# A graph network's layer-norm statistics merged, one copy moved from ScalarE to VectorE, and the instructions of all engines in a new order

## The chip, the cores and the metric

The kernel runs on one core of a Trainium2 chip. The metric is the device time of one execution in microseconds (us); several executions give a median. A separate, profiled execution left the trace that the views below read.

TensorE (PE) multiplies matrices, VectorE (DVE) and ScalarE (ACT) work element by element, GpSimd (POOL) does the powers of the layer norms, and SyncE (SP) starts most of the DMAs.

## The reference

64 graphs of 256 nodes with 256 features go through four layers. Every layer begins with a layer norm and a relu, and adds its result to its input. Layers 0 to 2 are graph attention (four heads, four heads with bias, relu and a norm of each head, and one head), layer 3 is a GRU of three steps over the neighbours' messages.

```python
h = jnp.maximum(_layernorm(x, axis=-1), 0.0)
x = x + _L0_gnn_ref(h, adj, ...)      # attention, 4 heads of 64, elu
h = jnp.maximum(_layernorm(x, axis=-1), 0.0)
x = x + _L1_gnn_ref(h, adj, ...)      # attention, 4 heads of 64, bias, relu, norm per head
h = jnp.maximum(_layernorm(x, axis=-1), 0.0)
x = x + _L2_gnn_ref(h, adj, ...)      # attention, 1 head of 256
h = jnp.maximum(_layernorm(x, axis=-1), 0.0)
x = x + _L3_gnn_ref(h, adj, ...)      # 3 GRU steps:
# m = h @ weight[i]; aggr = A^T @ m; r, z = sigmoid(..); n = tanh(i_n + r * h_n)
# h = (1 - z) * n + z * h
def _layernorm(x, axis=-1, eps=1e-5):
    m = jnp.mean(x, axis=axis, keepdims=True)
    v = jnp.var(x, axis=axis, keepdims=True)
    return (x - m) / jnp.sqrt(v + eps)
```

## The kernel before, in words

**Units.** The work comes in 33 units: the first and the last hold one graph, the 31 between hold two. A unit's rows are cut into chunks of 128 nodes (four for two graphs), and `graphs` (L1027) describes a unit's layers one after the other. `vec` (L879) wraps most VectorE operations and some of ScalarE's, so these all stand on L880 in the profile (L906 in the changed kernel) and are told apart by their tiles.

**Norm (L1041).** For each chunk VectorE takes `bn_stats` (L1048, six numbers per row: count, mean and spread of the even and of the odd elements) and `bn_aggr` (L1049, mean and variance). In layers 0 to 2 a small VectorE operation makes the row of negative means, ScalarE subtracts the mean and takes the relu (`xn`, L1063), another small one adds eps, and GpSimd's power makes the reciprocal root, which is applied later to the projected rows. Ahead of the GRU (`whole`) ScalarE's relu has the reciprocal root as its scale (L1069).

**Attention.** `xn` is transposed, by TensorE (L1104, units 0 to 2 and 32) or by DMA: ScalarE splits it into two planes of 16 bits (L1119), a transposing DMA turns the planes, and ScalarE joins them (L1125). TensorE projects (L1143). For each head `weights` (L1234) makes the attention's weights `pt`: in the plain form VectorE does four passes (L1240) and one minimum with the mask `cap`, over 128x1024; a head named in `LIFTED` has four ScalarE passes (L1249) and four shorter VectorE passes instead, but only in units of two graphs. TensorE then attends, two heads of 64 on half arrays (L1275, 128x64) or one head of 256 on the whole array.

**GRU (L1448).** TensorE's gates (L1492) multiply the state `ht` by `whh`, and the aggregated state `ag` by `wc`; ScalarE and VectorE make the gates from the banks. `split` (L1454) cuts a tile into a high and a low part, `hl`, and `aggregate` (L1464) multiplies both by the adjacency (L1471). Between two GRU steps the state is turned to rows, by TensorE (L1529) or, in units 1 to 31 for the first of the two 128-column halves and for both after the last step, in `rows_turned` (L1499): ScalarE splits planes (L1508), a DMA transposes them to `tp`, ScalarE joins them to `y` (L1513). `y` goes into `split` between steps, or is added to `xt` after the last.

**The order.** Every operation is first recorded with an engine, a cost in ns, and what it reads and writes. `_Schedule` (L555) then plays the engines through at build time. Due times are counted back from `sched.end` of a unit (L1603, a graph is given `PACE`/2), each engine takes the earliest due operation that is ready and has room in its pools, and `HOP` is the margin after an engine's operation before others may use its result. What it decides is the fixed order of the instructions on each engine and of the pools' slots; on the chip the instructions of an engine run in that order, and wait on semaphores.

Of the kernel before, what the change touches and what calls it, by code (L numbers as in the profile page):

```python
# [14 lines left out]
OP = mybir.AluOpType  # L15
# [509 lines left out]
BACK = range(1, 32)  # L525
EARLY = (0,)
LIFTED = (0,2)
LEAVE = 0
PACE = 98000.0

# [17 lines left out]
class _Op:  # L548
    __slots__ = (
        "engine", "cost", "port", "emit", "group", "bufs", "takes", "nbytes", "succs", "waits", "due", "ready",  # L550
        "index", "yields", "base", "grabs", "leave",
    )


class _Schedule:  # L555
# [11 lines left out]
    OVERLAP = {"pe": 0, "act": 97, "dve": 81, "pool": 0, "sp": 0}  # L567
    HOP = {"pe": 300, "act": 100, "dve": 200, "pool": 100, "sp": 0}
    DMA_LATENCY = 3500
# [5 lines left out]
    YIELD = 5000.0  # L575
    GUARDED = ()
    STRICT = ("hl",)

    def __init__(self, tc, pools):
# [11 lines left out]
    def op(self, engine, cost, emit, reads=(), writes=(), takes=(), nbytes=0, port=False, yields=False,  # L591
           grabs=False, leave=0):
        o = _Op()
        o.leave = leave
        o.port, o.yields, o.grabs = port or grabs, yields, grabs
        o.engine, o.base, o.emit, o.group, o.nbytes = engine, cost, emit, self.group, nbytes
        o.cost = cost * self.RESERVE.get(engine, 1.0)
        o.succs, o.index, o.ready = [], len(self.ops), 0.0
        deps, o.bufs, o.takes = set(), [], []
        for written, items in ((False, reads), (True, writes)):  # L600
            for item in items:
                b, part = item if isinstance(item, tuple) else (item, None)
                if b not in o.bufs:
                    o.bufs.append(b)
                    b.left += 1
                if written and b.tile is None and b not in o.takes:
                    o.takes.append(b)
                keys = list(b.parts) if part is None else [k for k in (part, None) if k in b.parts]
                for k in keys:
                    writer, readers = b.parts[k]  # L610
                    if writer is not None:
                        deps.add(writer)
                    if written:
                        deps.update(readers)
                writer, readers = b.parts.get(part, (None, []))
                if written:
                    if part is None:
                        b.parts.clear()
                    b.parts[part] = (o.index, [])
                else:  # L620
                    b.parts[part] = (writer, readers + [o.index])
        for b in takes:
            if b.tile is None and b not in o.takes:
                o.takes.append(b)
        deps.discard(o.index)
        o.waits = len(deps)
        for d in deps:
            self.ops[d].succs.append(o)
        self.ops.append(o)
        return o  # L630
# [55 lines left out]

    def run(self):
        ops = self.ops
        for o in reversed(ops):
            late = self.end[o.group]  # L690
            for s in o.succs:
                if s.group == o.group or o.group not in self.end or o.group < 0:
                    late = min(late, s.due - self.STRETCH * s.cost - self.MARGIN)
            if o.nbytes:
                late -= self.DMA_LATENCY + o.nbytes / self.DMA_RATE
            o.due = late
        self.started = set()
        self.takers = {c: [] for c in self.pools}
# [7 lines left out]
        clock = self.dma_free = self.port_free = 0.0  # L706
        kept, holder = False, None
        count = 0
# [14 lines left out]
        while True:  # L723
            for e in engines:
# [5 lines left out]
                if e == "pool":  # L730
                    kept = False
                while able[e]:
                    item = heapq.heappop(able[e])
                    o = ops[item[1]]
                    free = not o.port or self.port_free <= clock and not (o.yields and kept)
                    if e == "dve" and o.port and kept and spare(o.due + self.YIELD):
                        free = False
                    if o.yields and holder == "pool" and clock < self.port_free <= clock + 200:
                        free = True
                    if e == "pool" and not free and self.roomy(o):  # L740
                        kept = True
                    if free and self.roomy(o):
                        self.start(o, clock)
                        idle[e] = False
                        free = clock + o.cost - self.OVERLAP[e]
                        post(free, "free", o)
                        if o.grabs:
                            self.port_free, holder = clock + 100, e
                            post(clock + 100, "tick", o)
                        elif o.port and not (o.yields and self.port_free > clock):  # L750
                            self.port_free, holder = free, e
                            post(free - 200, "tick", o)
                        break
                    held.append(item)
                for item in held:
                    heapq.heappush(able[e], item)
# [27 lines left out]
def _fast_path(  # L784
# [242 lines left out]
    def graphs(u, first, nb):  # L1027
# [13 lines left out]
        def norm(xt, cls, whole):  # L1041
# [4 lines left out]
            def stats(c):  # L1046
# [3 lines left out]

                op("dve", 615, emit, [(xt, c)], [(st, c), (mv, c)])

# [3 lines left out]
            def centred(c):  # L1056
                to, view = part(c)
                if c in CENTRED:
                    vec(nc.vector.tensor_scalar, 410, view, lambda: xt.tile[:, c, :],
# [3 lines left out]
                op("act", 505, lambda: nc.scalar.activation(  # L1063
                    view(), xt.tile[:, c, :], AF.Relu, bias=mv.tile[:, 3, c : c + 1],
                ), [(xt, c), (mv, "b")], [to])

# [7 lines left out]
            for c in range(C):  # L1074
                stats(c)
            if not whole and not all(c in CENTRED for c in range(C)):
                vec(nc.vector.tensor_scalar, 150, lambda: mv.tile[:, 3, :], lambda: mv.tile[:, 0, :], -1.0, None,
                    op0=OP.mult, reads=parts(mv, range(C)), writes=[(mv, "b")])
            if not whole:
                for c in range(C):  # L1080
                    centred(c)
            vec(nc.vector.tensor_scalar, 150, lambda: mv.tile[:, 2, :], lambda: mv.tile[:, 1, :], 1e-5, None,
                op0=OP.add, reads=parts(mv, range(C)), writes=[(mv, "r")])
            vec(nc.gpsimd.tensor_tensor, 220 + 195 * C, lambda: mv.tile[:, 2, :], lambda: mv.tile[:, 2, :],
                nhalf[:, :C], op=OP.pow, writes=[(mv, "r")], engine="pool", grabs=True)
            if whole:
                vec(nc.vector.scalar_tensor_tensor, 160, lambda: mv.tile[:, 3, :], lambda: mv.tile[:, 0, :], -1.0,
                    lambda: mv.tile[:, 2, :], op0=OP.mult, op1=OP.mult,
                    reads=parts(mv, range(C)) + [(mv, "r")], writes=[(mv, "b")])
                for c in range(C):  # L1090
                    scaled(c)
            return xns, mv

        def transposed(xns, cls):
# [18 lines left out]
            def turned(b):  # L1113
                pl, tp = buf("pl", [P, 2, 2 * D], U16), buf("tp", [P, 2, 2 * D], U16)

                def planes(flat):
                    return flat.bitcast(U16).rearrange("p (n k) -> p k n", k=2)

                op("act", 1040, lambda: nc.scalar.copy(  # L1119
                    pl.tile, planes(xns[b].tile.rearrange("p c d -> p (c d)"))), [xns[b]], [pl])  # L1120
                dma("sp", 1 << 18, lambda: nc.sync.dma_start(
                    tp.tile.rearrange("p k (m n) -> p (k m) n", n=P), pl.tile.rearrange("p k n -> p (k n)"),
                    transpose=True,
                ), [pl], [tp], cost=1250)
                op("act", 1330, lambda: nc.scalar.copy(  # L1125
                    planes(ht.tile[:, 2 * b : 2 * b + 2].rearrange("p c d n -> p (c d n)")), tp.tile,
                ), [tp], [(ht, b)])

# [105 lines left out]
        def weights(cap, f, cbs, h):  # L1234
# [21 lines left out]

            if h in LIFTED and nb == 2:
                for b in range(nb):
# [21 lines left out]
        def attend_heads(o, o_view, pts, wh, hs):  # L1280
# [8 lines left out]

            op("pe", pe(958) * len(hs), emit, [*pts, wh], banks_, takes=[o])  # L1290

# [156 lines left out]
        def gru(pair):  # L1448
# [5 lines left out]
            def split(src, turned, reads, port=False):  # L1454

                hl = buf("hl", [P, 2, C, P] if turned else [P, 2, 2, D], F32R)
                op("act", act(590) if turned else 590,
                   lambda: nc.scalar.copy(hl.tile[:, 0], src()), reads, [(hl, 0)])  # L1458
                vec(nc.vector.tensor_tensor, dve(683) if turned else 683, lambda: hl.tile[:, 1], src,
# [39 lines left out]
            def rows_turned(ht, j, last):  # L1499
# [5 lines left out]
                def planes(flat):  # L1505
                    return flat.bitcast(U16).rearrange("p (n k) -> p k n", k=2)

                op("act", 1040, lambda: nc.scalar.copy(pl.tile, planes(ht.tile[:, j, :])), [(ht, j)], [pl])  # L1508
                dma("sp", 1 << 18, lambda: nc.sync.dma_start(
                    tp.tile.rearrange("p k (m n) -> p (k m) n", n=P), pl.tile.rearrange("p k n -> p (k n)"),  # L1510
                    transpose=True,
                ), [pl], [tp], cost=1250)
                op("act", 1330, lambda: nc.scalar.copy(  # L1513
                    planes(y.tile.rearrange("p c d -> p (c d)")), tp.tile), [tp], [y])
                if not last:
# [161 lines left out]
```

## Time and profile before

| | us |
|---|---|
| median of 3 runs | 3011.49 (3011.26 to 3012.68) |
| profiled execution: its own time | 3010.84 |
| its span | 3009.0 |
| TensorE (PE) busy | 2972.5 |
| ScalarE (ACT) busy | 2435.3 |
| VectorE (DVE) busy | 2286.4 |
| GpSimd (POOL) busy | 295.5 |

The largest groups of instructions say what each engine's time consists of. A line of this view names the code's line, the engine, the operation, the tile written and the tiles read, the shapes and the count; then the busy time in all, the mean of one in ns, and the idle time before.

```profile
L1492 PE MATMUL bank<-ag,wc 128*128 128x512 f32 (+1 forms) x2376 | 1061.6, 581 | 0.0
L1492 PE MATMUL bank<-ht,whh 128*128 128x512 f32 (+1 forms) x2376 | 1059.7, 580 | 0.8 <-ACT ht L880 0.8
L1275 PE MATMUL bank<-wh,pt 128*64 128x65 f32 (+1 forms) x8704 | 375.7, 232 | 1.7 <-ACT f L1229 1.2
L1048 DVE BATCH_NORM_STATS2 st<-xt 128x6 f32<-128x256 f32 x512 | 207.5, 405 | 5.9 <-DMA xt<-in_x_dram 5.9
L1049 DVE BATCH_NORM_AGGREGATE mv<-st 128x2 f32<-128x6 f32 x512 | 94.0, 184 | 19.9
L1513 ACT COPY y<-tp 128x1024 uint16<-128x1024 uint16 x124 | 163.9, 1334 | 0.0
```

Two thirds of TensorE's time are the GRU's gates. A group's busy time can be below count times mean, since instructions overlap a little. The chain of work that ended last is followed back from the last instruction; the windows give every engine's busy time in a stretch, and the clock granted to TensorE; the waits name what TensorE stood idle for; the timeline shows single instructions, or runs of them, with start and duration.

### The profile page before, as it was taken

To read this page: it belongs to the slowest core of one execution; us is meant where nothing else is said; L and a number is where in the kernel's file an instruction comes from. 1 tells how busy PE (TensorE), PEld (TensorE's weight loads), DVE (VectorE), ACT (ScalarE), POOL (GpSimd) and SP (SyncE) were. 2 spreads that over 40 slices of the span, in tenths; PEclk is the share of its full clock that TensorE was granted. 3 is DMA by queue.
4 is the path that set the end of the run, shared out by engine and by line. 5 is a ranking of instruction groups with operands and counts; after the bars stand their busy time and mean duration, and the time that the engine had idled before them with its cause. 6 is when DMAs were issued, how large, how long until landed. Compare 5 with 4: busy or idle time off the path is not lost.

```text
span 3009.0 us, 47645 instructions
## 1 busy us (share of the span) xinstructions
PE 2972.5 (99%) x17175; PEld 1780.5 (59%) x17175; DVE 2286.4 (76%) x5510; ACT 2435.3 (81%) x4445; POOL 295.5 (10%) x317
## 2 busy tenths in 40 slices
PE   8899999999999999999999999999999999999998
PEld 6765656556556555565556565555565555555556
DVE  7878877778877778777788777788777788777754
ACT  7877888878789797888878888787897978877654
POOL 2101000111100101010010100111001010100000
PEclk9999999999999999999999999999999999999999
DMA  4222333333333333333333234233333333322210
GB/s 137 67 67 58 88 74 85 92 65 92 73 86 94 78 78 75 91 79 81 84 71 96 67 85 101 59 92 78 88 85 81 78 74 86 69 60 67 46 37 19
DMA packets 494793, 232.12 MB, mean 77 GB/s; under 512 B 421642, under 2 KB 474452, under 8 KB 494548
## 3 DMA queue, kind: packets, MB, share of 16 engines
q1 hardware_dynamic: 490576, 227.62, 32.9%
q8 instruction: 138, 2.26, 0.3%
q10 hardware_dynamic: 3972, 1.36, 0.2%
q14 instruction: 107, 0.88, 0.1%
HBM read 109.84 MB, written 17.34 MB: 42 GB/s over the span
## 4 chain that ended last, share of the span: by engine, by line
PE 97%; DVE 2%; ACT 1%; DMA 0%; issue 0%; SPq 0%; ACTq 0%; DVEq 0%
PE bank L1492 66%; PE bank L1275 12%; PE bank L1143 11%; PE bank L1471 6%; PE bank L1529 1%; PE bank L1000 0%; PE bank L1198 0%; DVE o L880 0%; PE bank L1104 0%; DVE g L880 0%; DVE pt L880 0%; PE bank L1178 0%; DMA w0e<-in_L_gnn_W_dram 0%; DVE pt L1240 0%; ACT pt L1249 0%; DVE ht L880 0%
## 5 line engine op out<-in xcount | busy, mean ns | idle before, releaser
L1492 PE MATMUL bank<-ag,wc 128*128 128x512 f32 (+1 forms) x2376 | 1061.6, 581 | 0.0
L1492 PE MATMUL bank<-ht,whh 128*128 128x512 f32 (+1 forms) x2376 | 1059.7, 580 | 0.8 <-ACT ht L880 0.8
L1492 PEld LDWEIGHTS bank<-ag,wc 128*128 128x128 f32 x2376 | 444.6, 190 | 476.1 <-issue 451.3
L1492 PEld LDWEIGHTS bank<-ht,whh 128*128 128x128 f32 x2376 | 440.1, 191 | 470.8 <-issue 444.3
L880 ACT ACTIVATE g<-bank,bg 128x512 f32<-128x512 f32 (+1 forms) x594 | 393.1, 670 | 188.9 <-PE bank L1492 185.3
L880 DVE SCALAR_TENSOR_TENSOR g<-g,g 128x512 f32<-128x512 f32 (+1 forms) x396 | 266.3, 673 | 323.9 <-ACT g L880 322.2
L1275 PEld LDWEIGHTS bank<-wh,pt 128*64 128x64 f32 (+1 forms) x8704 | 343.5, 141 | 80.5 <-issue 58.3
L1275 PE MATMUL bank<-wh,pt 128*64 128x65 f32 (+1 forms) x8704 | 375.7, 232 | 1.7 <-ACT f L1229 1.2
L1249 ACT ACTIVATE pt<-cb,f 128x256 f32<-128x256 f32 x620 | 325.9, 591 | 0.4 <-PE bank L1275 0.4
L1125 ACT COPY ht<-tp 128x1024 uint16<-128x1024 uint16 x232 | 303.4, 1340 | 0.1
L880 DVE SCALAR_TENSOR_TENSOR pt<-pt,f,cap 128x256 f32<-128x256 f32 x620 | 275.0, 485 | 35.2 <-ACT pt L1249 34.5
L880 POOL TENSOR_TENSOR mv<-mv,nhalf 128x4 f32<-128x4 f32 (+1 forms) x132 | 142.0, 1076 | 1189.7 <-DVE mv L880 1178.6
L1471 PE MATMUL bank<-am_r,hl 128*128 128x256 f32 x1536 | 241.6, 307 | 0.7 <-ACT hl L1458 0.5
L1119 ACT COPY pl<-xn 128x1024 uint16<-128x1024 uint16 x232 | 233.9, 1040 | 0.0
L1471 PEld LDWEIGHTS bank<-am_r,hl 128*128 128x128 f32 x1536 | 198.8, 190 | 47.4 <-issue 37.3
L880 ACT ACTIVATE g<-g,bg 128x512 f32<-128x512 f32 (+1 forms) x198 | 139.3, 705 | 106.1 <-DVE g L880 105.8
L880 POOL TENSOR_TENSOR mean<-mean,nhalf 128x8 f32<-128x8 f32 (+1 forms) x66 | 134.9, 2063 | 788.2 <-DVE mean L880 755.5
L1048 DVE BATCH_NORM_STATS2 st<-xt 128x6 f32<-128x256 f32 x512 | 207.5, 405 | 5.9 <-DMA xt<-in_x_dram 5.9
L1153 ACT ACTIVATE wh<-bank,mv 128x264 f32<-128x264 f32 (+1 forms) x384 | 172.0, 479 | 43.1 <-PE bank L1143 41.6
L880 DVE SCALAR_TENSOR_TENSOR g<-ht,g 128x512 f32<-128x512 f32 (+1 forms) x198 | 132.4, 670 | 85.3 <-ACT g L880 85.1
L1240 DVE TENSOR_SCALAR pt<-cb,f 128x256 f32<-128x256 f32 x532 | 188.2, 410 | 6.5 <-ACT cb L1186 3.2
L880 DVE SCALAR_TENSOR_TENSOR g<-bank,g 128x512 f32<-128x512 f32 (+1 forms) x198 | 133.2, 673 | 72.5 <-PE bank L1492 67.0
(97 smaller groups left out, 3333.7 us busy)
## 6 DMA issues: line engine op xcount, KB each, us to landing
cb<-rd SPq DMA_DIRECT2D x120, 512.0 KB, 4.9
xt<-in_x_dram SPq DMA_DIRECT2D x31, 512.0 KB, 4.1
at<-in_adj_dram SPq DMA_DIRECT2D x31, 512.0 KB, 3.8
out_dram<-xt SPq DMA_DIRECT2D x31, 512.0 KB, 3.0
cb<-rd SPq DMA_DIRECT2D x34, 256.0 KB, 3.3
tp<-pl SPq DMA_TRANSPOSE x356, 3.1
cap<-cap_n SPq DMA_TRANSPOSE x128, 2.4
rd<-row ACTq DMA_DIRECT2D x60, 8.0 KB, 1.3
```

The lines of the kernel that those rows point to most:

```text
L880: emit = lambda: fn(*[a() if callable(a) else a for a in args], **kw)
L1048: nc.vector.bn_stats(st.tile[:, c, :], xt.tile[:, c, :])
L1119: op("act", 1040, lambda: nc.scalar.copy(pl.tile, planes(xns[b].tile.rearrange("p c d -> p (c d)"))), [xns[b]], [pl])
L1125: op("act", 1330, lambda: nc.scalar.copy(planes(ht.tile[:, 2 * b : 2 * b + 2].rearrange("p c d n -> p (c d n)")), tp.tile,), [tp], [(ht, b)])
L1143: nc.tensor.matmul(ps.tile[:, : heads * W], lhsT=ht.tile[:, c, dc, :], rhs=we[:, dc].rearrange("p h w -> p (h w)"), start=(dc == 0), stop= ...
L1153: op("act", 470, lambda: nc.scalar.activation(wh.tile[:, :, c, :], ps.tile[:, : heads * W].rearrange("p (h w) -> p h w", h=heads), AF.Iden ...
L1240: nc.vector.tensor_scalar(pt.tile[:, b, jc, :].rearrange("p (i n) -> p i n", n=P), cb.tile[:, k, 2 * b : 2 * b + 2, :], f.tile[:, 1, h, c ...
L1249: op("act", 590, lambda: nc.scalar.activation(view().rearrange("p (i n) -> p i n", n=P), cb.tile[:, k, 2 * b : 2 * b + 2, :], AF.Relu, sca ...
L1275: nc.tensor.matmul(ps[q * Q : (q + 1) * Q], lhsT=pt.tile[:, b, jc, i0 : i0 + Q], rhs=wh.tile[:, h, 2 * b + jc, :w], start=(jc == 0), stop= ...
L1471: nc.tensor.matmul(ps.tile[:, b * N : (b + 1) * N], lhsT=rows(k, b, sc), rhs=am.tile[:, 2 * b + sc, :], start=(k == 0 and sc == 0), stop=( ...
L1492: nc.tensor.matmul(by_chunk(ps.tile[:, :S]), lhsT=w[:, dc, g * P : (g + 1) * P], rhs=block(v, dc), start=(first and dc == 0), stop=(last a ...
L1529: nc.tensor.transpose(ps.tile[:, c * P : (c + 1) * P], ht.tile[:, j, c * P : (c + 1) * P], ident)
```

## The change

Four things are done.

1. `MERGED`: no `bn_aggr`. The spread and the means of the halves are merged for all chunks at once, by five small VectorE operations: the bias row (minus the sum of the two means, so that the relu takes twice `xt`), and four that give the variance with eps.
2. `JOIN_DVE = ("y",)`: the 124 joins of `y` are VectorE copies. The splits into planes, and the joins of `ht`, stay on ScalarE.
3. `LIFTED0 = (0,)` with `HEADS = 3`: units 0 to 2 lift head 0 alone, and units of one graph lift as well.
4. The planner: `HOP` of VectorE 60 ns for 200, `PACE` 97000 for 98000, pools `wh` and `cb2_` guarded, and the attends marked as `halves`, so that among TensorE operations of equal due time one of the same kind as the last is preferred (`STICK` and `SWITCH` are zero). The order of the instructions changes on every engine.

```diff
+HEADS = 3
+LIFTED0 = (0,)
+JOIN_DVE = ("y",)
+MERGED = True
 LIFTED = (0,2)
 LEAVE = 0
-PACE = 98000.0
+PACE = 97000.0
...
-    HOP = {"pe": 300, "act": 100, "dve": 200, "pool": 100, "sp": 0}
+    HOP = {"pe": 300, "act": 100, "dve": 60, "pool": 100, "sp": 0}
...
-    GUARDED = ()
+    GUARDED = ("wh","cb2_")
     STRICT = ("hl",)
+    STICK = 0.0
+    SWITCH = {True: 0.0, False: 0.0}
...
+                if MERGED:
+                    vec(nc.vector.bn_stats, 405, lambda: st.tile[:, c, :], lambda: xt.tile[:, c, :],
+                        reads=[(xt, c)], writes=[(st, c)])
+                else:
+                    op("dve", 615, emit, [(xt, c)], [(st, c), (mv, c)])
+
+            def merged():
+                m0, q0, m1, q1 = (st.tile[:, :, k] for k in (1, 2, 4, 5))
+                d, s, v = (mv.tile[:, k, :] for k in range(3))
+                share = 1.0 / D if whole else 4.0 / D
+                stt = nc.vector.scalar_tensor_tensor
+                nc.vector.tensor_tensor(d, m0, m1, op=OP.subtract)
+                stt(s, q0, 1e-5 * D, q1, op0=OP.add, op1=OP.add)
+                stt(d, d, 0.25 if whole else 1.0, d, op0=OP.mult, op1=OP.mult)
+                stt(v, s, share, d, op0=OP.mult, op1=OP.add)
...
                 op("act", 505, lambda: nc.scalar.activation(
                     view(), xt.tile[:, c, :], AF.Relu, bias=mv.tile[:, 3, c : c + 1],
+                    scale=2.0 if MERGED else 1.0,
                 ), [(xt, c), (mv, "b")], [to])
...
+            if MERGED:
+                vec(nc.vector.scalar_tensor_tensor, 165, lambda: mv.tile[:, 3, :], lambda: st.tile[:, :, 1], -1.0,
+                    lambda: st.tile[:, :, 4], op0=OP.mult, op1=OP.subtract,
+                    reads=parts(st, range(C)), writes=[(mv, "b")])
...
+            if MERGED:
+                op("dve", 560, merged, parts(st, range(C)), [(mv, "r")])
...
+        def planes_op(by_dve, cost, to, of, reads, writes):
+            if by_dve:
+                vec(nc.vector.tensor_copy, 690, to, of, reads=reads, writes=writes, port=True)
+            else:
+                op("act", cost, lambda: nc.scalar.copy(to(), of()), reads, writes)
...
-            if h in LIFTED and nb == 2:
+            if h in (LIFTED if u >= HEADS else LIFTED0):
...
-            op("pe", pe(958) * len(hs), emit, [*pts, wh], banks_, takes=[o])
+            op("pe", pe(958) * len(hs), emit, [*pts, wh], banks_, takes=[o], halves=True)
...
-                op("act", 1330, lambda: nc.scalar.copy(
-                    planes(y.tile.rearrange("p c d -> p (c d)")), tp.tile), [tp], [y])
+                planes_op("y" in JOIN_DVE, 1330, lambda: planes(y.tile.rearrange("p c d -> p (c d)")),
+                    lambda: tp.tile, [tp], [y])
```

## The prediction

> **What bounds the kernel now.** I read the page's busy shares and its chain first, then the table of windows, TensorE's waits, and its timeline where it idles.
>
> ```profile
> PE 2972.5 (99%) x17175; PEld 1780.5 (59%) x17175; DVE 2286.4 (76%) x5510; ACT 2435.3 (81%) x4445; POOL 295.5 (10%) x317
> PE 97%; DVE 2%; ACT 1%; DMA 0%; issue 0%; SPq 0%; ACTq 0%; DVEq 0%
> ```
>
> TensorE is busy for 2972.5 of 3009.0 us and is 97% of the chain. The windows show where the other 36.5 us lie:
>
> ```profile
> 25.00:50.00 25.00, 24.44 (x287) 20.75 (x288) 21.24 (x73) 24.18 (x72) 3.31 (x5) 1.00 0.38 110
> 75.00:100.00 25.00, 15.78 (x305) 14.09 (x304) 23.64 (x65) 21.14 (x60) 2.28 (x4) 0.94 0.38 96
> 100.00:125.00 25.00, 24.21 (x120) 21.07 (x120) 23.06 (x63) 18.71 (x48) 4.60 (x5) 0.85 0.07 22
> ...
> 1410.00:1504.00 94.00, 94.00 (x533) 55.22 (x533) 71.18 (x173) 83.26 (x159) 8.02 (x10) 1.00 0.40 92
> 2820.00:2914.00 94.00, 91.94 (x403) 49.66 (x403) 58.76 (x143) 56.79 (x90) 5.34 (x7) 1.00 0.21 49
> 2914.00:3008.00 94.00, 84.80 (x329) 55.84 (x327) 35.16 (x75) 39.87 (x72) 0.80 (x2) 0.99 0.08 20
> ```
>
> Columns: length, busy time of TensorE, its loads, VectorE, ScalarE, GpSimd; then the clock. From 282 to 2820 us TensorE never idles. Of the start's 24.2 us idle (first 300 us), 9.2 fall between 75 and 100 us, where VectorE is busy 23.64 of 25, and the clock stands at 0.94 and 0.85. The end has 11. The waits and the timeline name the causes:
>
> ```profile
> PE bank L1104 <- ACT xn L1063: 9.4, 1, 9.4
> PE bank L1104 <- ACT xn L1069: 7.5, 1, 7.5
> ...
> 99.79 1.18 PE L1104 MATMUL bank<-ident,xn 128*128 128x128 f32 x4 [7.47 <-ACT xn L1069]
> 101.77 3.78 PE L1492 MATMUL bank<-ht,whh 128*128 128x256 f32 x8 [0.79 <-ACT ht L880]
> ```
>
> The first GRU gate, 8 matmuls of 256 columns, starts at 101.77 and takes 3.78 us; the same form takes 1.89 later: half clock, recorded from 97.1 to 107.3 us. So VectorE and ScalarE bound about 100 us, TensorE's work bounds 2700, latency the last 100. A mean load of 76% and 81% says little; only what shortens the start, the end or TensorE's own work moves the time.
>
> **Part by part.** *Statistics.* 512 aggregates (184 ns) and 231 TENSOR_SCALAR (164 ns) go: 94.2+37.9 = 132.1 us. Five small passes for each of 132 norms come: 660 at the 165 ns of the same small rows = 108.9. By durations VectorE saves 23 us. Here a rule speaks against the change: the Trainium skill ("VectorE: DVE Perf Modes", "Rules for kernel authors") counts operations, since each empties the pipe. For four chunks that is 10 before and 9 after (10 and 10 in the norm ahead of the GRU): almost nothing. The trace shows more than a count:
>
> ```profile
> 15.13 0.41 DVE L1048 BATCH_NORM_STATS2 st<-xt 128x6 f32<-128x256 f32 x1
> 15.58 0.18 DVE L1049 BATCH_NORM_AGGREGATE mv<-st 128x2 f32<-128x6 f32 x1
> 15.68 0.39 DVE L1048 BATCH_NORM_STATS2 st<-xt 128x6 f32<-128x256 f32 x1
> 16.11 0.18 DVE L1049 BATCH_NORM_AGGREGATE mv<-st 128x2 f32<-128x6 f32 x1
> ```
>
> A pair repeats every 0.55 us, because the aggregate starts only when its statistics have ended; operations that don't feed each other follow at their duration less 0.08, here 0.32. So before: 4×0.55+2×0.08 = 2.36; after: 3×0.32+0.46 (a dependent start) + about 0.6 for five = 2.0. I take 0.35 us of queue per norm, 46 in all; by the rule it is 10 or less. Neither shows in the middle, where VectorE is loaded to 75%.
>
> *Joins.* 124 copies `y<-tp` leave ScalarE (1.334 us, 165.4 in all). VectorE has no row for them. Nearest below: the one-source cast `am_r<-am`, 128x1024, 0.695; nearest above: the two-source `pt<-pt,cap`, 128x1024, 1.226. The skill's same page ("What auto-detection actually checks") gives double rate to one source between two SBUF tiles with even outer dimensions, as here; but ScalarE needs 1.340 to write 2-byte values apart against 1.040 to read them so, and VectorE might pay too. I take 0.69, nearest in kind: +86 us; by the upper row +152. Behind the wait for the transposed planes stand the GRU's VectorE passes, and behind those TensorE's banks; a transpose lands 3.1 us after issue, and the order allows for 4.7. Cover: between the end of `hl<-y,hl` and its aggregate I find 0.73, 0.98, 1.64 and 2.01 us, so even 1.226 (0.54 over the plan) stays covered.
>
> *Heads.* Units 1 and 2 drop head 2's ScalarE lift in two layers: 4×(4×0.410+1.226−4×0.485) = +3.7 us VectorE, −9.4 ScalarE. Eight one-graph heads gain it: −4.3, +9.5. Sums: VectorE 2286−23+86−1 = 2348 (78%; at most 2414, 80%), ScalarE 2435−165 = 2270 (75%). In the middle both stay under TensorE.
>
> *New order, middle.* TensorE's instructions are as many and of the same forms. Runs between the half-array attends (128*64) and the rest fall from 181 to 155. The timeline prices one:
>
> ```profile
> 1423.37 1.88 PE L1492 MATMUL bank<-ht,whh 128*128 128x512 f32 x4
> 1425.18 3.95 PE L1275 MATMUL bank<-wh,pt 128*64 128x65 f32 x128
> 1429.07 1.98 PE L1492 MATMUL bank<-ag,wc 128*128 128x512 f32 x4
> 1430.89 1.45 PE L1492 MATMUL bank<-ht,whh 128*128 128x512 f32 x3
> ```
>
> From start to start the gate before the attends takes 1.81 us and the one after 1.82, against 1.716 between gates elsewhere: 0.1 a switch, 26×0.1 = −2.6. The planner's VectorE margin falls from 200 to 60 ns, so products come sooner after what they wait for: TensorE's work between a unit's `ag` and its product is at least 1.71 us (1.73 before), for `hl` 2.66 (2.58), for the transposes of `ht` 3.45 (3.93); those of `wh` mostly 1.71 instead of 3.43, a distance at which before has no idle. I take +1 for stalls, bounds 0 and +10.
>
> *Start.* TensorE's first matmul waits on ScalarE's first relu (table load); unchanged. Ahead of the split for the first aggregate (real start 102.70) VectorE's queue holds 84.8 us of work in before, 78.1 in after (every instruction ahead in the order, by its form's time from start to start), and 18.4 of idle. If that idle stays, the split comes at 96.5 and the first gate near 97; if DMA or ScalarE set it, at 101; if all queues shorten alike (ScalarE's is 81.4, then 72.3), at 94. Counted in the same way TensorE has 63.55 us of work before that gate, in after 61.6 (four projections of unit 3, 3.56 us, now stand inside the gap; other work moved behind). Lost time is start less work: 38.2 before, 97−61.6 = 35.4 after, so −2.8, bounds +1.2 and −5.8. Half clock cost 3.5 us (lost time grew by 4.3 from 99.8 to 112, 0.8 of it idle). The projections split the gap, and the end's 1.80-us wait didn't lower the clock; no row shows how short is short enough, so I take half, −1.8, bounds 0 and −3.5.
>
> *End.* Where before waits 0.26 and 1.80 us on `ht` (2828, 2911), TensorE's work in between grows from 1.84 and 0.44 to 3.94 and 2.17; the projections put there have short waits of their own. In the last, one-graph unit the order saves some 0.5. I take −1.5, bounds +1 and −3.
>
> **Sum.** −2.6+1−2.8−1.8−1.5 = −7.7 us. The profiled run took 3010.84 (span 3009.0 and 1.84 outside it) and lies 0.65 under the median 3011.49; I carry the difference to the median: 3003.8.
>
> **Rivals.** *Hidden anyway (0.21).* What is relieved lies beneath a busy TensorE, and the start's gap is set by DMA and ScalarE: the timeline has ScalarE waiting on DMA and on `o` near 91 and 94 us. Then only the switches stay, less a stall or two: 3008 to 3012. *Slower: the join comes late (0.17).* The margin gives 0.14 of the cover away, so it decides from a join of 0.69+0.73−0.14 = about 1.3 us on. At 1.7 the closest cover is passed by some 0.4 us; if all 62 middle joins sit so close, `L1471` waits 62×0.45 = 28 us in all, and the time is 3032; with half of them, 3018. For it: ScalarE's 1.34 for the same strided write. Against it: both VectorE rows lie under 1.3. *The start goes well (0.18).* Gate at 94 and no half clock: −2.6−5.8−3.5−3 = −15, or 2996. *The change doesn't do what it says*: excluded for the instructions, which I counted in the built order; only their times are open.
>
> **Chances.** Forecast (3000 to 3008) 0.44; well 0.18; hidden 0.21; slower 0.17. A measurement here can tell 0.2%, 6.0 us, from no change. Faster (under 3005.5): 0.38 of the forecast's case and 0.18 = 0.56; same: 0.06+0.21 = 0.27; slower (over 3017.5) 0.17. The range 2994 to 3016 leaves out the slower case and a little of the best.
>
> **What would show it.** Right: join rows near 0.69 us; statistics 0.32 apart; middle windows still full; the gap before the first gate under 5 us; gate start near 97; ScalarE near 2270. Wrong: joins over 1.2 and waits of `L1471` on `hl`, idle TensorE between 282 and 2820 us, or a first gate after 101 with the clock still halved.

## The result, and the profile after

The changed kernel takes 3004.84 us (median of 16 runs, 3003.15 to 3006.78); the kernel before, run beside it, 3011.03 (16 runs, 3009.95 to 3012.68). The ratio is 0.998 with a 95% interval of 0.9972 to 0.9987: 6.2 us faster (3.9 to 8.4), where the prediction had 3003.8. The profiled execution took 3004.92 us, its span is 3003.1.

First the busy times and the chain from the page, as before:

```profile
PE 2969.4 (99%) x17175; PEld 1783.2 (59%) x17175; DVE 2330.5 (78%) x5547; ACT 2313.0 (77%) x4321; POOL 279.5 (9%) x317
PE 98%; DVE 1%; ACT 0%; DMA 0%; issue 0%; SPq 0%; ACTq 0%; DVEq 0%
```

ScalarE lost 122 us and VectorE gained 44; the time moved by 6. TensorE's busy time fell by 3.1 us with the same 17175 instructions, its idle time from 36.5 to 33.7. The windows that answer to those of before (length, busy TensorE, its loads, VectorE, ScalarE, GpSimd, then the clock):

```profile
25.00:50.00 25.00, 24.53 (x273) 20.88 (x272) 19.17 (x61) 20.73 (x60) 2.12 (x5) 0.97 0.36 106
75.00:100.00 25.00, 18.42 (x247) 14.69 (x247) 24.97 (x63) 20.02 (x49) 4.57 (x5) 0.96 0.25 65
100.00:125.00 25.00, 24.76 (x185) 21.70 (x185) 23.47 (x75) 20.82 (x55) 3.19 (x4) 0.97 0.31 96
...
1410.00:1504.00 94.00, 94.00 (x535) 54.62 (x534) 76.85 (x184) 78.77 (x149) 7.75 (x9) 1.00 0.37 85
2820.00:2914.00 94.00, 93.00 (x425) 52.62 (x424) 57.46 (x143) 54.35 (x100) 6.27 (x9) 1.00 0.17 38
```

Between 75 and 100 us TensorE is busy 18.42 us for 15.78. VectorE is not relieved there: at 24.97 of 25 it is now full. The middle has no visible idle time, as before. TensorE's timeline around the first gate:

```profile
87.98 1.13 PE L1200 MATMUL bank<-w0e,ht 128*128 128x264 f32 x4 [0.37 <-DVE o L906]
90.03 2.02 PE L1200 MATMUL bank<-w0e,ht 128*128 128x264 f32 x8 [0.92 <-DVE xt L906]
92.57 1.16 PE L1200 MATMUL bank<-w0e,ht 128*128 128x264 f32 x4 [0.51 <-ACT wh L1210]
94.78 0.28 PE L1255 MATMUL bank<-ident,wh 128*16 128x128 f32 x1 [1.06 <-ACT wh L1210]
96.20 0.93 PE L1161 MATMUL bank<-ident,xn 128*128 128x128 f32 x4 [1.13 <-ACT xn L1112]
97.95 3.68 PE L1553 MATMUL bank<-ht,whh 128*128 128x256 f32 x8 [0.82 <-ACT ht L906]
```

The single wait of 7.47 us is cut into several of about 1 us by unit 3's projections. The first gate starts at 97.95 instead of 101.77. Its 3.68 us for a form that takes 1.89 show half clock again; the clock record has it for 3.4 us here (98.1 to 101.5) instead of 10.2, but for another 3.4 at 23 us, where before had none.

**Where the 5.9 us of span went.** A wait shorter than the profile resolves shows as a slightly longer busy row, so I made a ledger that counts it. I give each TensorE instruction the usual time from its start to the next one's (a four-matmul gate 1.716 us); the sum is 2919.2 us for both kernels. An instruction's start less the sum of all ahead of it is the time lost up to there: waiting, half clock and switches between half-array attends and the rest. A run of one kind, in the table, is the work between two switches. The losses are those up to 272 us, from there to 2880, and after, in each kernel's own profiled execution (work and the three losses give the span); the other kernels are the experiments below:

| kernel | runs of one kind | start | middle | end | span | median |
|---|---|---|---|---|---|---|
| before | 181 | 46.2 | 28.4 | 15.3 | 3009.0 | 3011.03 |
| after | 155 | 43.5 | 25.5 | 15.0 | 3003.1 | 3004.84 |
| f_aggr | 155 | 46.0 | 30.8 | 15.1 | 3011.0 | 3013.26 |
| f_join_part | 155 | 44.2 | 36.8 | 15.6 | 3015.7 | 3017.01 |
| f_join2 | 155 | 43.2 | 58.1 | 16.0 | 3036.5 | 3039.11 |
| anti2000 | 231 | 44.5 | 36.3 | 14.5 | 3014.5 | 3016.02 |
| nopace | 247 | 42.5 | 38.2 | 13.7 | 3013.6 | 3017.42 |
| u_merge | 183 | 49.1 | 36.6 | 15.4 | 3020.2 | 3020.15 |
| u_join | 215 | 42.0 | 60.0 | 15.2 | 3036.3 | 3037.51 |
| u_heads | 151 | 44.3 | 22.4 | 14.7 | 3000.6 | 3004.85 |
| u_plan | 231 | 48.5 | 43.2 | 15.6 | 3026.5 | 3027.92 |
| b_stick | 147 | 48.2 | 25.1 | 18.0 | 3010.5 | 3011.28 |
| o_plan | 171 | 43.9 | 85.0 | 27.5 | 3075.6 | 3077.50 |
| gathered | 143 | 43.3 | 24.8 | 15.3 | 3002.6 | 3003.22 |

The change gained 2.7 us at the start, 2.9 in the middle, 0.3 at the end. These are one execution of each kernel. The changed kernel, f_join_part and f_join2 have the same instructions in the same order up to the first join at 181.9 us; their starts lost 43.2 to 44.2 us, and their first gates came at 97.95, 98.16 and 96.83. So an edge is known to a us or so.

### The profile page after: what moved, and what is told of

It reads as the page before. It is cut to its first block, busy times and chain, and to the rows that moved or that the text cites. A ratio compares the mean times of both kernels' runs of the same rounds, so it can differ in the third digit from the quotient of the medians.

```text
span 3003.1 us, 47684 instructions
## 1 busy us (share of the span) xinstructions
PE 2969.4 (99%) x17175; PEld 1783.2 (59%) x17175; DVE 2330.5 (78%) x5547; ACT 2313.0 (77%) x4321; POOL 279.5 (9%) x317
## 4 chain that ended last, share of the span: by engine, by line
PE 98%; DVE 1%; ACT 0%; DMA 0%; issue 0%; SPq 0%; ACTq 0%; DVEq 0%
PE bank L1553 66%; PE bank L1332 12%; PE bank L1200 12%; PE bank L1532 6%; PE bank L1590 1%; PE bank L1026 1%; PE bank L1235 0%; PE bank L1161 0%; PE bank L1255 0%; DMA w0e<-in_L_gnn_W_dram 0%; DVE o L906 0%; DVE g L906 0%; ACT g L906 0%; DVE xt L906 0%; DVE ht L906 0%
## 5 line engine op out<-in xcount | busy, mean ns | idle before, releaser
L1532 PE MATMUL bank<-am_r,hl 128*128 128x256 f32 x1536 | 251.5, 312 | 0.0
L906 DVE BATCH_NORM_STATS2 st<-xt 128x6 f32<-128x256 f32 x512 | 183.1, 411 | 7.0 <-DMA xt<-in_x_dram 6.0
L906 POOL TENSOR_TENSOR mean<-mean,nhalf 128x8 f32<-128x8 f32 (+1 forms) x66 | 114.6, 1743 | 739.4 <-DVE mean L906 714.3
L1105 ACT ACTIVATE xn<-xt,mv 128x256 f32<-128x256 f32 x384 | 167.5, 496 | 4.9 <-DVE mv L906 4.1
L906 ACT COPY ag<-bank 128x512 f32<-128x512 f32 (+1 forms) x198 | 109.0, 566 | 79.9 <-PE bank L1532 79.6
```

The source lines that it names most:

```text
L906: emit = lambda: fn(*[a() if callable(a) else a for a in args], **kw)
L1105: op("act", 505, lambda: nc.scalar.activation(view(), xt.tile[:, c, :], AF.Relu, bias=mv.tile[:, 3, c : c + 1], scale=2.0 if MERGED else 1 ...
L1532: nc.tensor.matmul(ps.tile[:, b * N : (b + 1) * N], lhsT=rows(k, b, sc), rhs=am.tile[:, 2 * b + sc, :], start=(k == 0 and sc == 0), stop=( ...
```

## The experiments

Theory A: the gain is fewer switches and a shorter start, and the load taken from or put on VectorE and ScalarE counts nothing in the middle. Theory B, its rival: the relief itself counts there. The first three keep every instruction of the changed kernel in its place, so that the order can't be the cause; only VectorE has added work.

**f_aggr: the aggregates put back, in the changed order.**

```diff
+    spare_mv = consts.tile([P, 2], F32, name="spare_mv")
...
+                    def both():
+                        nc.vector.bn_stats(st.tile[:, c, :], xt.tile[:, c, :])
+                        nc.vector.bn_aggr(spare_mv[:, 0:2], st.tile[:, c, :])
-                    vec(nc.vector.bn_stats, 405, ...)
+                    op("dve", 405, both, [(xt, c)], [(st, c)])
```

> The changed kernel with every instruction in its place, and one bn_aggr put back behind each bn_stats (into a spare tile that nothing reads), so VectorE gets some 94 us of work and some 0.23 us of queue for each of 512 chunks back while the order stays. Theory A (relief counts only where TensorE waits, in the first 100 us): 24 such pairs stand ahead of the split for the first GRU gate, up to 24*0.23 = 5.5 us; the gate comes 2 to 5.5 us later, the time is 3007 to 3010, and between 282 and 2820 us nothing changes. Theory B (VectorE's relief also counts in the middle): 488 further chunks, 112 us of queue, show at least in part, say a quarter: 3030.

Measured 3013.26, ratio to before 1.0009 (1.0 to 1.0018): 8.4 over the changed kernel. The first gate comes 1.5 us later (99.40), less than A's 2 to 5.5, and the start loses 2.5. The middle loses 5.3, which A excludes: some 0.05 us per us of VectorE's queue, mostly ahead of aggregates (their `hl` late by about 0.1 us, 34 times). B's 25 is far off too. So in this order most of the 112 us stays hidden in the middle, but not all of it.

**f_join2 and f_join_part: a longer join, in the changed order.**

```diff
+                def twice():
+                    nc.vector.tensor_copy(to(), of())
+                    nc.vector.tensor_copy(to(), of())
-                vec(nc.vector.tensor_copy, 690, to, of, ...)
+                op("dve", 690, twice, reads, writes, port=True)
```

In f_join_part the second copy covers half the planes: `to()[:, :, : 2 * P]`, `of()[:, :, : 2 * P]`.

> The changed kernel with every instruction in its place, and each of the 124 joins of y done twice, so that a join costs 1.4 us where the order counts on 0.69. Theory A: the first join comes after the start, and the cover of 0.7 to 2 us ahead of the aggregates takes nearly all of it: 3004.8 to 3006. Theory B (the prediction's slower rival: a join over 1.3 us is past its cover): 62 aggregates wait some 0.3 us or more, L1532 waits on hl in every unit, 3020 or more.

> The changed kernel with every instruction in its place, and each join of y followed by a second copy of half its planes, some 0.35 us more, so that a join takes about 1.08 us where the order counts on 0.69 (the doubled one took 0.65 more and cost 34 us). Theory A (cover with an edge: the first 0.3 us are hidden, what lies beyond shows): 3005 to 3011. Theory B (no cover left, every 0.1 us of a join shows in the gates behind it): 34*0.35/0.65 = +18, so 3023.

f_join2: 3039.11, ratio 1.0095 (1.0079 to 1.011), 34 us over the changed kernel, 33 of them in the middle. f_join_part: 3017.01, ratio 1.0018 (1.0009 to 1.0027), 12 us over. f_join2 refutes A. In f_join_part both miss: 3011 at most and 3023 were expected. The added time was larger than both reckoned, too: from a join's start to VectorE's next it is 0.63 us in the mean in the changed kernel, 1.12 in f_join_part and 1.41 in f_join2, so 0.49 and 0.78 more. The place differs from the one that the prediction named. Three of TensorE's longest waits in f_join2 (engine and line, what ended the wait; us in all, times, longest), then one of f_join_part:

```profile
PE bank L1557 <- DVE o L906: 11.4, 12, 1.0
PE bank L1336 <- DVE g L906: 6.9, 24, 0.4
PE bank L1594 <- DVE ht L906: 5.8, 8, 1.5
```

```profile
PE bank L1557 <- DVE o L906: 6.2, 12, 0.5
```

No aggregate (L1536 there) is among the large ones. TensorE's order is the same in all three, so each step from one start to the next can be compared with the changed kernel's. In the middle, of f_join_part's 11.3 us more, 8.1 lie at the 12 gates that wait for `o`; of f_join2's 32.8, 13.4 lie there, 11.0 at 24 attends (L1336), which wait for a bank until VectorE has read it for `g`, and 2.0 at aggregates. A gate (L1557) waits for a bank that an attend had used, until VectorE's multiplication to `o` has read it. VectorE's timeline shows that multiplication behind the join, and TensorE's the gate, at the same instructions in the changed kernel and in f_join2. The changed kernel:

```profile
1005.72 0.24 DVE L906 RECIPROCAL rs<-bank 128x4 f32<-128x4 f32 x2
1005.88 0.71 DVE L906 COPY y<-tp 128x1024 uint16<-128x1024 uint16 x1
1006.48 0.74 DVE L906 TENSOR_TENSOR o<-bank,rs 128x256 f32<-128x256 f32 x2
```

```profile
1007.69 1.88 PE L1553 MATMUL bank<-ht,whh 128*128 128x512 f32 x4
```

And f_join2, VectorE and then TensorE:

```profile
1015.60 0.24 DVE L906 RECIPROCAL rs<-bank 128x4 f32<-128x4 f32 x2
1015.76 0.72 DVE L1148 COPY y<-tp 128x1024 uint16<-128x1024 uint16 x1
1016.51 0.74 DVE L1149 COPY y<-tp 128x1024 uint16<-128x1024 uint16 x1
1017.14 0.74 DVE L906 TENSOR_TENSOR o<-bank,rs 128x256 f32<-128x256 f32 x2
```

```profile
1017.69 1.96 PE L1557 MATMUL bank<-ht,whh 128*128 128x512 f32 x4 [0.95 <-DVE o L906]
```

The join just ahead of the gate is not alone. A unit has three joins, and VectorE hardly catches up between them (by 0.14 us here). How far single instructions of this unit lie behind the same ones of the changed kernel (us):

| | f_join_part | f_join2 |
|---|---|---|
| TensorE and VectorE ahead of the first join (987.02 in the changed kernel) | 3.84 | 8.44 |
| VectorE behind the first join | 4.33 | 9.23 |
| VectorE behind the second (995.02) | 4.82 | 10.01 |
| VectorE behind the third (1005.88), so at the multiplication | 5.17 | 10.65 |
| TensorE just ahead of the gate | 3.85 | 8.89 |
| TensorE at the gate (1007.69) | 4.52 | 10.00 |

At the gate VectorE is 1.32 and 1.76 us further behind than TensorE, and TensorE waits 0.67 and 1.11 of them: 0.65 is covered in both, for three joins together, not for each. The attends stand behind two joins. In f_join2 VectorE is 1.56 behind there and they wait 0.4 to 0.6; in f_join_part it is 0.98 behind, and they don't wait. The other units of the middle repeat these numbers nearly; the gate waits in every second one.

**anti2000 and nopace: more switches.** In anti2000 TensorE prefers, within 2 us of due time, the kind that the last was not; nopace has the pace of before.

```diff
-    STICK = 0.0
+    STICK = 2000.0
...
-                        if best is None or o.halves == halves:
+                        if best is None or o.halves != halves:
...
-                            if e != "pe" or o.halves == halves:
+                            if e != "pe" or o.halves != halves:
```

```diff
-PACE = 97000.0
+PACE = 98000.0
```

> The changed kernel, but among TensorE operations whose due times lie within 2 us the order prefers the other kind (half-array attends against all else): 231 runs of one kind instead of 155, the same work. Theory A (a switch costs 0.1 us): 76*0.1 = +7.6, so 3012.4, spread evenly over the middle, with TensorE still busy throughout. Theory B (switches cost nothing, and what the order saved was waits): 3004 to 3006.

> The changed kernel planned with PACE 98000 as before, all else as changed: 247 runs of one kind instead of 155. Theory A: +9.2 from the switches, with the start's gap 0 to 3 us either way: 3011 to 3017, which is all of the change's gain given back. Theory B (the pace only moves due times, the gain came from the relief of VectorE and ScalarE): 3003 to 3007.

Measured 3016.02 (ratio 1.0015, 1.0006 to 1.0024) and 3017.42 (1.0022, 1.0013 to 1.0031): 11.2 and 12.6 us over the changed kernel, more than A's price and far from B. The page's busy row of anti2000, and one place of TensorE's timeline:

```profile
PE 2980.0 (99%) x17175; PEld 1781.0 (59%) x17175; DVE 2329.2 (77%) x5547; ACT 2297.8 (76%) x4321; POOL 275.1 (9%) x317
```

```profile
545.91 2.09 PE L1332 MATMUL bank<-wh,pt 128*64 128x65 f32 x64
547.93 1.98 PE L1553 MATMUL bank<-ag,wc 128*128 128x512 f32 x4
549.84 2.09 PE L1332 MATMUL bank<-wh,pt 128*64 128x65 f32 x64
```

The changed kernel has both groups of 64 in one row of 3.96 us here. The gate between them takes 1.91 us from start to start, 0.2 over its usual 1.716: a switch in and a switch out. The same instructions are busy 10.6 us longer and idle 34.5 us in place of 33.7, so it is not waiting. In the ledger's middle, 76 runs more cost 10.8 us and 92 more cost 12.7: 0.14 us each. The attends pay as well. The instruction behind them tells when they made way, in anti2000 and then, undivided, in the changed kernel:

```profile
551.86 2.94 PE L1200 MATMUL bank<-w0e,ht 128*128 128x264 f32 x12
```

```profile
546.51 3.96 PE L1332 MATMUL bank<-wh,pt 128*64 128x65 f32 x128
550.40 2.01 PE L1200 MATMUL bank<-w2e,ht 128*128 128x258 f32 x8
```

From start to start 64 attends take 2.02 us twice in anti2000, and 128 in one run 3.89 (the medians of all such runs in the middle of both are the same): dividing them costs 0.15. With the gate's 0.2 that makes about 0.17 a switch. Between 272 and 2880 us the change has 27 switches fewer, worth 4.6 us by this price (an estimate); the middle gained 2.9, so part of it must have been lost to waits too short to show.

**u_merge, u_join, u_heads, u_plan: one part undone, planned anew.**

```diff
-MERGED = True
+MERGED = False
```

```diff
-JOIN_DVE = ("y",)
+JOIN_DVE = ()
```

```diff
-            if h in (LIFTED if u >= HEADS else LIFTED0):
+            if h in LIFTED and nb == 2:
```

u_plan has `HOP` of VectorE 200, `PACE` 98000, no `GUARDED`, no `halves`.

> The changed kernel without the merged statistics (bn_aggr for each chunk, as before), planned anew: 183 runs of one kind on TensorE. The two runs with more switches and TensorE never idle in the middle put a switch at about 0.13 us. Theory A (the time follows the number of switches, and the start): 28*0.13 = +3.6, and the start up to 3 us later: 3008 to 3012. Theory B (the relief of VectorE is what counts): with the order fixed the aggregates cost 8.4 us, so 3013, whatever the switches.

> The changed kernel with the joins of y back on ScalarE, planned anew: 215 runs of one kind. Theory A: 60*0.13 = +7.8, start within 2 us: 3011 to 3015. Theory B (relief of ScalarE counts, VectorE's load costs): the joins' 91 us leave VectorE, which lies nearer to its limit than ScalarE, so the middle gains up to 5 us and the time is 3000 to 3005.

> The changed kernel with heads 0 and 2 lifted in units of two graphs alone, as before, planned anew: 151 runs of one kind. Theory A: -0.5 from the switches; units 0 to 2 give ScalarE 10 us of work back in the start, which moves the first gate by up to 3 us: 3003 to 3008. Theory B (the lifted heads of the first and last units made the gain): 3009 or more.

> The changed kernel with the planner as before (margin 200, PACE 98000, no guarded pools), planned anew: 231 runs of one kind. All relief stays in. Theory A: 76*0.13 = +9.9, start within 2 us, so 3013 to 3017, slower than before. Theory B: the relief made the gain and the planner's numbers little, 3003 to 3007.

| kernel | median | over the changed kernel | ratio to before |
|---|---|---|---|
| u_merge | 3020.15 | +15.3 | 1.003 (1.0019 to 1.0042) |
| u_join | 3037.51 | +32.7 | 1.0089 (1.0075 to 1.0102) |
| u_heads | 3004.85 | 0.0 | 0.998 (0.9971 to 0.9989) |
| u_plan | 3027.92 | +23.1 | 1.0056 (1.0042 to 1.007) |

Only u_heads lies where a theory put it (A): the heads show nothing in the median. In its profiled execution, the fastest of its 11, the middle loses 3.1 us less than the changed kernel's with 4 runs fewer. So the order also moves waits too short to show, by about as much as the whole middle gained, and the middle's 2.9 alone would not prove the switches; the rows above do. The other three miss both, and are slower than the kernel before. The ledger says why: u_merge and u_plan lose 5.6 and 5.0 us at the start, and in the middle, which loses 11, 34 and 18 us more, switches at 0.14 us explain 4, 8 and 11. Most of the rest are waits that neither before nor the changed kernel has. In u_join, for example (waits, then ScalarE's timeline and TensorE's):

```profile
PE bank L1553 <- ACT ag L906: 11.1, 11, 1.1
```

```profile
1150.93 1.98 ACT L1149 COPY pl<-xn 128x1024 uint16<-128x1024 uint16 x2
1152.82 0.57 ACT L906 COPY ag<-bank 128x512 f32<-128x512 f32 x1
```

```profile
1153.44 1.98 PE L1553 MATMUL bank<-ag,wc 128*128 128x512 f32 x4 [1.05 <-ACT ag L906]
```

The copy that a gate needs stands behind two splits into planes on ScalarE.

The start can be read in the same way. u_plan has all the relief and the planner as before, and its long gap is there still:

```profile
102.92 1.18 PE L1161 MATMUL bank<-ident,xn 128*128 128x128 f32 x4 [7.75 <-ACT xn L1112]
```

Its first gate comes at 104.92, later than before's 101.77. With the planner's settings alone (o_plan, next) it comes at 99.25; in u_merge, which has all but the merged statistics, at 99.75. So the new order divides the gap. The merged statistics may bring some 1.5 us more, as f_aggr has it too, but that is little above what one execution can tell, and each of these orders is another one.

**o_plan and b_stick: the kernel before with one thing of the planner.** o_plan has the four planner settings of the changed kernel and nothing else of it. b_stick is before with the preference for the last kind:

```diff
+    STICK = 5000.0
...
-            op("pe", pe(958) * len(hs), emit, [*pts, wh], banks_, takes=[o])
+            op("pe", pe(958) * len(hs), emit, [*pts, wh], banks_, takes=[o], halves=True)
```

> The kernel before with the planner's numbers of the changed one alone (margin 60, PACE 97000, guarded pools): 171 runs of one kind. Statistics, joins and heads as before. Theory A (switches and start alone): -1.3 from ten switches, start within 2 us: 3008 to 3012. Theory B (the planner's numbers fit only the relieved engines: with the tight margin and the joins on ScalarE the middle waits as in the run with the joins put back, some 28 us): 3025 to 3040.

> The kernel before in all but one thing: among TensorE operations whose due times lie within 5 us the order prefers the kind of the last (half-array attends or all else). 147 runs of one kind instead of 181, statistics, joins, heads, margin and pace as before. Theory A (0.13 us a switch, the start as before): 34*0.13 = -4.4, so 3006.6, nearly the change's gain with nothing moved between engines. Theory B (an order that wasn't drawn for it brings new waits in the middle, as with the parts undone): 3011 or more.

o_plan: 3077.50, ratio 1.0218 (1.0204 to 1.0232), 66 us over the kernel before, where B had some 28. Its longest waits in all, then one of them on TensorE and VectorE:

```profile
PE bank L1590 <- DVE mv L906: 36.9, 13, 3.0
```

```profile
1061.63 0.63 PE L1590 MATMUL bank<-ident,ht 128*128 128x128 f32 x4 [3.02 <-DVE mv L906]
```

```profile
1060.82 0.66 DVE L906 SCALAR_TENSOR_TENSOR ht<-g,g 128x512 f32<-128x512 f32 x1
```

`mv` is only the last before it on VectorE's queue: at 1061.63 us the transposes wait 3.02 us for `ht`, whose pass (1060.82) stands on VectorE behind layer 2's updates and four pairs of `bn_stats` and `bn_aggr`, which wait in turn for the attends that TensorE does from 1054.86 on. So the planner's numbers alone lose far more in the middle than they gain at the start; that short statistics and joins on VectorE are what makes them fit is likely, but was not tried one by one.

b_stick: 3011.28, ratio 0.9999 (0.999 to 1.0008). Its middle loses 25.1 us against 28.4: 3.3 us less for 34 switches, with 1.7 us of new visible waits in it (at 2775 and 2828 us), so near A's 4.4. But in the profiled execution the start loses 2.0 more, with the first gate at 103.11, and the end 2.7 more: among its waits one of 2.33 us on `ht` at 2910.51 against 1.80, and half clock for 3.4 us behind it. The gain is made and given back.

**gathered: the changed kernel with fewer switches.** `PACE` 96250 and `STICK` 5000.

> The changed kernel with PACE 96250 and the preference for the last kind within 5 us of due time: 143 runs of one kind instead of 155, the fewest of some 70 orders built. Theory A: 12*0.13 = -1.6, start within 2 us: 3001 to 3005. Theory B (each new order brings its own waits, of which the count of switches tells nothing): 3006 or more.

Measured 3003.22 (8 runs, 3001.98 to 3004.43), ratio to before 0.9973 (0.9963 to 0.9984), the fastest median of all. It is 1.6 us under the changed kernel's, but the two were not run side by side and their ranges overlap: A's size, not shown beyond doubt.

## Why the prediction was right or wrong, point by point

**Bound.** Right: TensorE stayed the bound, in the middle without a visible wait, while 122 us left ScalarE and 44 came to VectorE. That VectorE's queue does not show in the middle is a little too strong: in f_aggr 112 us of it cost 5.3.

**Costs of the parts.** Statistics: forecast 2.0 us a norm of four chunks; the middle's timeline has them in one piece:

```profile
1376.81 1.40 DVE L906 BATCH_NORM_STATS2 st<-xt 128x6 f32<-128x256 f32 x4
1378.24 0.17 DVE L906 SCALAR_TENSOR_TENSOR mv<-st 128x4 f32<-128x4 f32 x1
1378.33 0.16 DVE L1088 TENSOR_TENSOR mv<-st 128x4 f32<-128x4 f32 x1
1378.40 0.16 DVE L1089 SCALAR_TENSOR_TENSOR mv<-st 128x4 f32<-128x4 f32 x1
1378.52 0.16 DVE L1090 SCALAR_TENSOR_TENSOR mv<-mv 128x4 f32<-128x4 f32 x1
1378.71 0.16 DVE L1091 SCALAR_TENSOR_TENSOR mv<-mv 128x4 f32<-128x4 f32 x1
```

From 1376.81 to about 1378.8 is 2.0. Joins: 0.735 us in the mean, next to the nearer bound, by their group:

```profile
L906 DVE COPY y<-tp 128x1024 uint16<-128x1024 uint16 x124 | 91.1, 735 | 0.0
```

VectorE has 2330.5 us, for 2348 forecast; ScalarE 2313.0 for 2270, since the count took the joins' whole durations off: the durations of all ScalarE instructions fell by 174 us, but they overlap each other by 52 us less than before, and busy time counts an overlap once.

**Cover of the joins.** This step failed, unseen in the result: "so even 1.226 stays covered". I measured the cover where the join's own data go (0.73 to 2 us ahead of the aggregate), for one join at a time, and named the banks behind it without measuring theirs. f_join_part and f_join2 show that a bank runs out first, and that three joins share 0.65 us of cover there. A join at the upper row would have taken about 0.5 us more from start to start (0.55 by the row's duration); between the measured 12 us for 0.49 and 34 for 0.78 that makes some 13 to 17 us, an estimate, and the time 3018 to 3022, outside the range. The sum held because the join came out near the lower row, which the prediction took as the nearest in kind but had no measurement of; with the upper one, which it called covered, it would not have. To that extent it was luck.

**Switches.** Right in kind, the price too low: 0.1 forecast, 0.14 (anti2000 and nopace) to 0.17 measured. The prediction read the gates on either side, 1.81 and 1.82 us for 1.716, and left out what the attends between them pay. 26 fewer are then worth 3.6 to 4.4 us, for 2.6.

**Middle.** +1 forecast for stalls. None shows as idle, but the middle gained 2.9 for the 3.6 to 4.4 that the switches are worth, so by that estimate some 1 us of waits is in it: the term would have the right size. Both terms together, −1.6, are too small by 1.3. How clean the middle is depends on the order: the same parts in the orders of anti2000, nopace and u_plan lose 11 to 18 us more there, in that of gathered 0.7 less.

**Start.** −4.6 forecast, −2.7 measured. The gate: forecast at 97, came at 97.95, so its term is 38.2−36.3 = −1.9 for −2.8. Half clock: −1.8 forecast; behind the gate, up to 112 us, lost time grew by 2.0 us where it had grown by 2.8, so −0.8. The gate came near its forecast, but the new order did more for it than the lighter load: with the load lightened and the old planner (u_plan) it came at 104.92. The spell at 23 us, which before had not, stands inside the gate's term: at 60 us the changed kernel had lost 1.1 us more than before.

**End.** −1.5 forecast, −0.3 measured. The two places that I named did lose their waits; others of 1.14, 1.52 and 0.68 us stand in the changed kernel (2933, 2969 and 2905 us).

**Sum.** −7.7 forecast; −5.9 in the spans, −6.2 in the medians: start and end too large by 3.1 in all, the middle too small by 1.3. These errors partly cancel; the sum is nearer than its terms.

**Rivals.** Hidden anyway: wrong, the start did shorten, by more than its us of uncertainty, though mostly by the new order. Late join: its mechanism exists, at a lower edge and another place than it said; the join's 0.735 us is short enough. The start goes well: not so, the gate came at 97.95 and not at 94, and half clock came with it.

## What to carry to other kernels

When one engine is busy 99% of the time, look for work that it does without being told: here a change of array shape costs it 0.14 to 0.17 us, and the order decides how often. Cover must be measured at every wait behind an instruction on its queue, above all where it frees a buffer that the bound engine needs, not just along its own data; and if the instruction comes several times ahead of that wait, what is added to it counts as often. And an order drawn by a planner is one draw: undoing a single part of this change moved the time by 0 to 33 us, and no count of busy time told which.

## What the runs showed that I had not expected

Half clock comes with short gaps. In the profiled execution of o_plan TensorE waits 3.03 us for `ht` every second unit, 12 times, and the clock record has nine spells of 3.4 us between 407 and 2374 us, each beginning within 1.3 us of such a wait's end; the other three brought none. In b_stick a gap of 2.33 us was followed by one, in before the gap of 1.80 us was not. The changed kernel's waits of about 1 us each between 88 and 98 us still brought one. How short a gap is safe wasn't settled.

The planner's margin, pace and pools, changed alone, cost the kernel before 66 us, twice the most that undoing one part of the change cost. How much of it falls to each setting was not tried.
